# The FFN's residual addition moves from VectorE to a unit-matrix product on TensorE and a ScalarE copy

## The chip, the cores and the metric

The kernel runs on one core of one Trainium2 chip. The metric is the device time of one launch in microseconds (us), taken as the median of several executions. Five engines work side by side, each executing its own instructions in a fixed order and waiting on semaphores for the others: TensorE (PE in the profile), VectorE (DVE), ScalarE (ACT), GpSimd (POOL) and SyncE (SP), which here only issues DMA transfers.

## The reference, cut to what matters

The input x has 8 batches of 512 tokens with 256 channels, all in float32. Four blocks follow one another, each with a residual: a Mamba layer with its feed-forward network (FFN), a gated recurrence over the 8 batches, an attention, and the recurrence again. The change lies in the first block:

```python
h = layernorm(x, ln1_g, ln1_b)
h = h + mamba_mixer(rmsnorm(h, rms_w), ...)
x = x + h
h2 = layernorm(x, ln2_g, ln2_b)
x = x + (jax.nn.relu(h2 @ ffn_w1 + ffn_b1) @ ffn_w2 + ffn_b2)
```

It is the last of these lines: the FFN's second product, 512 tokens by 1024 hidden channels times 1024 by 256, is added to x. The reference's own outer residual adds the input once more, so the kernel's x collects all of it. The recurrence that follows takes the layer norm of this x.

## The kernel before, in words

The work of the first block, together with the first recurrence, fills the first 790 us of the 1630 us and is called the scan stage here. Each batch lies in one SBUF tile `cx.X[b]` of 128 partitions by 4 chunks of 256 channels; a chunk is 128 tokens. The order of nearly everything in the stage is written out by hand: `SLOTS`, `LAST` and `REST` are lists of short names, which `mamba_and_recurrence` walks from left to right, and every engine executes its own share of the resulting stream in that order.

A **period** below is one walk through the 16 slots, numbered by the batch whose scan it contains. In period b the scan of batch b runs (`scan`, `da0`, `da1`, `bx`, `y`, `ld`), and beside it pieces of its neighbours: `i.` and `e.` prepare batches b+1 and b+2, `o.` does the output projection and the FFN of batch b-1, `r.` and `q.` the recurrence of batches b-1 and b-2. Periods 0 to 6 follow `SLOTS`, period 7 follows `LAST`, and `REST` afterwards finishes batch 7 alone, in two halves.

One slot of the scan takes two scans (line 424) and two multiplications (line 428) on VectorE, two exponentials `da` on ScalarE (line 408), and one product `bx` on GpSimd (line 415). The `da` tiles lie in three PSUM banks, so an exponential waits until the scan of three units before has been done.

The FFN of one batch goes like this. `up0` to `up7` are the first product: each is four matmuls of 256 columns (line 517), and `up0_` to `up7_` are its bias and ReLU on ScalarE (line 530, two instructions each). `up0` to `up3` belong to chunks 0 and 1, `up4` to `up7` to chunks 2 and 3. `down0` to `down3` are the second product, one for each chunk of 128 tokens: eight matmuls of 256 columns which add up in one PSUM bank (line 541). `add0` to `add3` add that bank to the chunk of x (line 551), on VectorE. When all four are done, `r.stats` takes the statistics for the recurrence's layer norm (line 70, one instruction for each chunk, then lines 72, 94 and 83), and `r.norm` on ScalarE, `r.turn0`, `r.turn1` and the gates `r.f0` and so on follow. The chunks are worked in the order 1, 0, 3, 2.

Earlier in the same period GpSimd has added the FFN's output bias (`o.bias`, line 479) and the FFN's input (`o.residual`, line 483) to x, so `add` is the last step on x in this block.

The second product, the turns, the gates and the first product share three PSUM banks (tag `mm`); each new product waits until the one that used its bank has been read. In `SLOTS` the pieces around the change stand as follows (slots 8 to 13, shortened):

```python
... i.dt0
da0 o.up3_ i.dt0_ i.soft_exp bx o.down1 da1 o.down0 scan o.add1 ld
ld scan e.outer i.soft_rest da0 o.up4 i.soft_ln o.add0 c.gate0 o.up5 y bx o.up7 o.up4_ da1 o.up6 o.up5_ e.affine o.up6_
i.soft o.up7_ da0 da1 scan bx i.store_dx q.output0 o.down3 o.down2 o.add3 ld
e.square scan da0 o.add2 da1 ld bx y
da0 r.stats q.output0_ q.g1 q.output1 ...
```

Names that come up later: `i.soft_exp` (lines 326 to 328) and `i.soft_ln` (line 337) are ScalarE's part of the next batch's softplus, `i.soft_rest` (lines 332, 333) GpSimd's, and `i.soft` (lines 343, 344) VectorE's; their results are stored and then spread over the partitions by the DMAs `ld`. `e.outer` is four ScalarE instructions (line 106), `e.square` four more (line 205). `c.gate0` is line 453 and 456. `q.output0` and `q.output1` (line 704) exist only in periods 2 and 3. `i.rms` begins with one small VectorE instruction (line 83, tile `ve_a_r`).

Of the kernel before, what the change touches and what calls it, by code (L numbers as in the profile page):

```python
# [87 lines left out]
def layernorm_scales(cx, x, name, scales=((1.0, EPS),)):  # L88

    nc = cx.nc  # L90
    m = x.shape[1]
    mv = token_stats(cx, x, name)
    neg = cx.small.tile([P, TC], F32, tag="neg", name=f"neg_{name}")
    nc.vector.tensor_scalar_mul(neg[:, :m], mv[:, :, 0], -1.0)
    r = inv_sqrt(cx, mv[:, :, 1], scales, name)
    nb = cx.small.tile([P, len(scales), TC], F32, tag=f"nb{len(scales)}", name=f"nb_{name}")
    for i in range(len(scales)):
        nc.gpsimd.tensor_mul(nb[:, i, :m], neg[:, :m], r[:, i, :])
    return [(r[:, i, :], nb[:, i, :m]) for i in range(len(scales))]


def normalize(cx, out, x, scales):

    r, nb = scales
    for c in range(x.shape[1]):
        cx.nc.scalar.activation(
            out[:, c, :], x[:, c, :], AF.Identity, bias=nb[:, c : c + 1], scale=r[:, c : c + 1]
        )


def to_channels(cx, src, k, ps, chunks=range(TC)):

    for i, c in enumerate(chunks):
        cx.nc.tensor.transpose(ps[:, ts(c, P)], src[:, i, ts(k, P)], cx.ident)
    return ps


def part_of(half):

    if half is None:  # L120
        return "", slice(0, L), slice(0, TC)
    tokens, chunks = (slice(half * n // 2, (half + 1) * n // 2) for n in (L, TC))
    return "." + "ab"[half], tokens, chunks
# [322 lines left out]
def mamba_out(cx, a, t, b):  # L446

    nc, v = cx.nc, cx.v
    n = f"o{b}"

    def gate_out(k):

        nc.vector.scalar_tensor_tensor(
            t.y[k], t.xc[:, k, :], v["D"][:, k : k + 1], t.y[k], ALU.mult, ALU.add
        )
        nc.vector.tensor_mul(t.zs[:, k, :], t.zs[:, k, :], t.y[k])

    def proj(i):

        c0 = 2 * i  # L460
        ps = cx.psum.tile([P, 2, E], F32, tag="mm", name=f"ps_op_{n}_{c0}")
        for i in range(2):
            for k in range(KC):
                nc.tensor.matmul(
                    ps[:, i, :],
                    t.zs[:, k, ts(c0 + i, P)],
                    a.out_proj[:, k, :],
                    start=(k == 0),
                    stop=(k == KC - 1),
                )  # L470
        t.proj[c0] = ps

    def add_proj(half):
        for h in range(2) if half is None else [half]:
            u = t.u[:, ts(h, 2), :]
            nc.vector.tensor_add(u, u, t.proj[2 * h])

    def bias():
        nc.gpsimd.tensor_add(t.x, t.x, cx.rows3["ffn_b2"])

    def residual(half):
        cs = part_of(half)[2]
        nc.gpsimd.tensor_add(t.x[:, cs, :], t.x[:, cs, :], t.u[:, cs, :])

    def stats(half):
        t.scales[half] = layernorm_scales(cx, t.u[:, part_of(half)[2], :], n + part_of(half)[0])

    def norm(half):
        if not half:
            t.un = cx.tok.tile([P, TC, E], F32, tag="h", name=f"un_{n}")  # L490
            t.h2 = cx.ch.tile([P, KC, L], F32, tag="T", bufs=3, name=f"h2_{n}")
        cs = part_of(half)[2]
        normalize(cx, t.un[:, cs, :], t.u[:, cs, :], t.scales[half][0])

    def turn(k, half):
        on, _, cs = part_of(half)
        ps = cx.psum.tile([P, L], F32, tag="mm", name=f"ps_h2_{n}_{k}{on}")
        t.ps["h2", k, half] = to_channels(cx, t.un[:, cs, :], k, ps, chunks=range(TC)[cs])

    def turn_(k, half):  # L500
        tk = part_of(half)[1]
        nc.scalar.activation(
            t.h2[:, k, tk],
            t.ps["h2", k, half][:, tk],
            AF.Identity,
            bias=v["b2"][:, k : k + 1],
            scale=v["g2"][:, k : k + 1],
        )

    def up(i):  # L510

        half, m0 = i // 4, i % 4 * 2
        ps = cx.psum.tile([P, 2, L // 2], F32, tag="mm", name=f"ps_f_{n}_{i}")
        t.ps["up", i] = ps
        for m in range(2):
            for k in range(KC):
                nc.tensor.matmul(  # L517
                    ps[:, m, :],
                    a.w1[:, k, ts(m0 + m, P)],
                    t.h2[:, k, ts(half, L // 2)],  # L520
                    start=(k == 0),
                    stop=(k == KC - 1),
                )

    def up_(i):
        half, m0 = i // 4, i % 4 * 2
        if m0 == 0:
            t.f = cx.ch.tile([P, FC, L // 2], F32, tag="f", bufs=1, name=f"f_{n}_{half}")
        for m in range(2):
            nc.scalar.activation(  # L530
                t.f[:, m0 + m, :],
                t.ps["up", i][:, m, :],
                AF.Relu,
                bias=v["ffn_b1"][:, m0 + m : m0 + m + 1],
            )

    def down(c):

        ps = cx.psum.tile([P, E], F32, tag="mm", name=f"ps_f2_{n}_{c}")
        for m in range(FC):  # L540
            nc.tensor.matmul(  # L541
                ps,
                t.f[:, m, ts(c % 2, P)],
                a.w2[:, m, :],
                start=(m == 0),
                stop=(m == FC - 1),
            )
        t.down[c] = ps

    def add(c):  # L550
        nc.vector.tensor_add(t.x[:, c, :], t.x[:, c, :], t.down[c])

    t.proj, t.down, t.scales = {}, {}, {}
    pieces = {"bias": bias}
    for name, f, count in (
        ("gate{}", gate_out, KC), ("proj{}", proj, 2), ("up{}", up, 8), ("up{}_", up_, 8),
        ("down{}", down, TC), ("add{}", add, TC),
    ):
        for i in range(count):
            pieces[name.format(i)] = lambda f=f, i=i: f(i)  # L560
    for half in (None, 0, 1):
        on = part_of(half)[0]
        for f in (add_proj, residual, stats, norm):
            pieces[f.__name__ + on] = lambda f=f, half=half: f(half)
        for name, f in (("turn{}", turn), ("turn{}_", turn_)):
            for i in range(KC):
                pieces[name.format(i) + on] = lambda f=f, i=i, half=half: f(i, half)
    return pieces
# [272 lines left out]
o.bias y o.gate1 o.proj0 o.add_proj.a q.g1 o.stats.a o.residual.a o.norm.a o.proj1 o.turn0.a  # L841
o.turn1.a o.add_proj.b o.turn0_.a o.stats.b o.turn1_.a q.g1_ o.up0 o.norm.b o.up1 q.output1_ o.up2
o.up0_ o.up1_ o.turn1.b o.up3 o.up2_ o.turn1_.b o.up3_ o.turn0.b o.down1 o.down0 o.turn0_.b o.up4
o.residual.b o.up4_ o.up6 q.update1 o.up5 o.up5_ o.up7 o.add1 o.up6_ o.up7_ o.add0 o.down3 o.add3
o.down2 r.stats.a o.add2 r.norm.a r.stats.b
""".strip().split("\n")

# [764 lines left out]
```

## Time and profile before

| what | value |
|---|---|
| median of 3 runs | 1631.15 us (1631.02 to 1632.5) |
| profiled execution | 1632.17 us |
| its span, first to last instruction | 1630.4 us |
| TensorE busy | 1483.8 us (91% of the span) |
| VectorE busy | 1180.8 us (72%) |
| ScalarE busy | 885.2 us (54%) |
| GpSimd busy | 528.7 us (32%) |
| mean granted TensorE clock | 0.95 |

The shares are averages over stages with different limits: from 220 to 580 us both TensorE and VectorE are busy for some 83 to 85 us of every 90, while after 760 us VectorE has little to do. In a timeline each row has the start, the time that the merged instructions took, the engine, the line, the operation, the tiles and the shapes, and in square brackets the idle time before it with what ended it. In a chain each row is one piece of the chain of waits that ended last, with its start and its length. A float32 matmul stands in the records as two instructions.

### The profile page before, as it was taken

Reading aid. Unit: us, or ns where it says so; the run is one execution under the profiler, and the core shown is the slowest. Engines: PE = TensorE matmul, PEld = TensorE weight load, DVE = VectorE, ACT = ScalarE, POOL = GpSimd, SP = SyncE. Lnnn points to the kernel's source line nnn. Section 1 sums busy time; section 2 is a strip of 40 time slices with the busy share of each in tenths; the row PEclk is TensorE's granted clock in tenths of the full one; section 3 lists DMA queues with packets and bytes.
Section 4 is the critical chain, followed back from the end, with each engine's and each line's share of the span. In section 5 each row is a group of like instructions: output and inputs, shape, how many; then the busy total and the mean of one; then the engine's idle time right before and its main releaser. Section 6 shows DMA issues by size and latency. Waiting matters only on the chain.

```text
span 1630.4 us, 19741 instructions
## 1 busy us (share of the span) xinstructions
PE 1483.8 (91%) x6804; PEld 708.6 (43%) x6804; DVE 1180.8 (72%) x1674; ACT 885.2 (54%) x1338; POOL 528.7 (32%) x307
## 2 busy tenths in 40 slices
PE   4347979999999989999989999999999999999998
PEld 1103636455554646456734443333333333333346
DVE  3699998989899898973476867665666657655435
ACT  5775858686767666542235545454444544454422
POOL 2576767767585855541220000000000000000000
PEclk8656989999999999999989999999999999999999
DMA  6979897989989788960211110101010010100123
GB/s 209 254 199 249 205 241 177 281 208 254 245 212 235 206 221 207 227 160 1 107 53 38 43 23 27 27 15 32 13 33 17 26 24 27 27 12 23 29 94 129
DMA packets 111300, 196.04 MB, mean 120 GB/s; under 512 B 16480, under 2 KB 27040, under 8 KB 111200
## 3 DMA queue, kind: packets, MB, share of 16 engines
q1 hardware_dynamic: 108912, 187.79, 44.1%
q10 hardware_dynamic: 1824, 5.15, 0.9%
q0 software_dynamic: 464, 1.84, 0.3%
q8 instruction: 54, 0.88, 0.2%
q14 instruction: 46, 0.38, 0.1%
HBM read 159.06 MB, written 23.07 MB: 112 GB/s over the span
## 4 chain that ended last, share of the span: by engine, by line
PE 64%; DVE 19%; ACT 5%; DMA 5%; issue 4%; POOL 2%; SPq 1%; DVEq 0%; ACTq 0%; POOLq 0%
PE ps_s_c L1111 10%; PE ps_e_c L1111 9%; DVE hc_a L424 8%; PE ps_o_c L1157 8%; DMA dl_rep_a<-dl_dram_a 4%; DVE hc_a L428 3%; PE ps_f_o L517 3%; PE ps_f_o L541 2%; PE ps_v_c L1080 2%; PE ps_w_c L1198 2%; PE ps_f_d L593 2%; PE ps_i_d L593 2%; PE ps_g_d L593 2%; PE ps_f_d L602 2%; PE ps_g_d L602 2%
## 5 line engine op out<-in xcount | busy, mean ns | idle before, releaser
L1122 DVE TENSOR_REDUCE mp<-ps_s_c 128x2 f32<-128x1024 f32 x256 | 301.8, 1220 | 180.1 <-PE ps_s_c L1111 180.1
L1148 ACT ACTIVATE e_c<-ps_e_c 128x1024 f32<-128x1024 f32 x256 | 248.6, 1021 | 166.5 <-PE ps_e_c L1111 166.3
L415 POOL TENSOR_TENSOR bx_a<-dx_rep_a,B_a 128x1024 f32<-128x1024 f32 x128 | 301.6, 2367 | 105.5 <-DVE hc_a L424 68.6
L424 DVE TENSOR_TENSOR_SCAN hc_a<-da_a,bx_a 128x512 f32<-128x512 f32 x256 | 298.2, 1204 | 5.9 <-ACT da_a L408 4.5
L408 ACT ACTIVATE da_a<-dl_rep_a,neg_a 128x512 f32<-128x512 f32 x256 | 173.3, 688 | 147.5 <-DVE hc_a L424 97.0
L1111 PE MATMUL ps_s_c<-keys,q_c 32*128 32x512 f32 x1024 | 176.3, 643 | 2.9 <-ACT q_c L1074 1.2
L1111 PE MATMUL ps_e_c<-q_c,keys 32*128 32x512 f32 x1024 | 164.5, 639 | 2.2 <-DVE mp L1122 2.2
L428 DVE TENSOR_TENSOR hc_a<-hc_a,Cp_a 128x512 f32<-128x512 f32 x256 | 160.7, 667 | 0.0
L1157 PE MATMUL ps_o_c<-e_c,va 128*32 128x512 f32 x1024 | 138.0, 605 | 0.4 <-ACT oT_c L1173 0.3
L84 POOL TENSOR_TENSOR rs_d<-ve_d,neg_half 128x4 f32<-128x4 f32 x8 | 8.1, 1014 | 351.5 <-DVE ve_d L83 351.5
L517 PE MATMUL ps_f_o<-h_o,w 128*128 128x256 f32 x512 | 121.2, 386 | 0.7 <-ACT f_o L530 0.3
L541 PE MATMUL ps_f_o<-w,f_o 128*128 128x256 f32 x512 | 114.2, 381 | 3.8 <-ACT f_o L530 3.8
L437 PE MATMUL y_a<-hc_a,sum 128*32 128x512 f32 x512 | 91.7, 696 | 23.4 <-DVE hc_a L428 15.3
L517 PEld LDWEIGHTS ps_f_o<-h_o,w 128*128 128x128 f32 x512 | 96.6, 192 | 35.0 <-issue 10.3
L541 PEld LDWEIGHTS ps_f_o<-w,f_o 128*128 128x128 f32 x512 | 96.3, 190 | 22.9 <-ACT f_o L530 5.4
L1111 PEld LDWEIGHTS ps_s_c<-keys,q_c 32*128 32x128 f32 x1024 | 57.3, 183 | 94.3 <-issue 39.4
L84 POOL TENSOR_TENSOR rs_c<-ve_c,neg_half 128x4 f32<-128x4 f32 x7 | 7.1, 1009 | 264.9 <-DVE ve_c L83 264.9
L1111 PEld LDWEIGHTS ps_e_c<-q_c,keys 32*128 32x128 f32 x1024 | 50.9, 183 | 93.7 <-issue 59.8
L240 PE MATMUL ps_in_a<-hT_a,w_in 128*128 128x512 f32 x128 | 69.6, 683 | 1.1 <-ACT hT_a L235 1.1
L530 ACT ACTIVATE f_o<-ps_f_o,vecs 128x256 f32<-128x256 f32 x128 | 52.1, 468 | 23.0 <-PE ps_f_o L517 20.2
L1157 PEld LDWEIGHTS ps_o_c<-e_c,va 128*32 128x32 f32 x1024 | 20.4, 108 | 90.0 <-issue 78.5
L1190 DVE RECIPROCAL sum_c<-sum_c 128x256 f32<-128x256 f32 x32 | 55.7, 1742 | 1.2 <-DMA sum_c<-oT_c 1.2
(327 smaller groups left out, 2146.8 us busy)
## 6 DMA issues: line engine op xcount, KB each, us to landing
dl_rep_a<-dl_dram_a SPq DMA_DIRECT2D x256, 256.0 KB, 6.4
dx_rep_a<-dx_dram_a SPq DMA_DIRECT2D x256, 256.0 KB, 6.4
x<-in_x_dram SPq DMA_DIRECT2D x8, 512.0 KB, 9.6
keys<-xT_c SPq DMA_DIRECT2D x128, 32.0 KB, 1.9
o_c<-oT_c SPq DMA_DIRECT2D x128, 32.0 KB, 1.9
sum_c<-oT_c SPq DMA_DIRECT2D x128, 32.0 KB, 2.0
xT_dram_d<-xT_d SPq DMA_DIRECT2D x8, 512.0 KB, 2.8
xT_back<-xT_dram_d SPq DMA_DIRECT2D x8, 512.0 KB, 5.5
```

Source lines behind the costliest of these rows:

```text
L408: cx.nc.scalar.activation(t.da[u], t.dl_rep[u // 2][:, u % 2, :], AF.Exp, scale=a.A[:, u : u + 1])
L415: cx.nc.gpsimd.tensor_mul(t.bx[pair], t.dx_rep[pair], t.B.unsqueeze(1).to_broadcast([P, 2, L]))
L424: cx.nc.vector.tensor_tensor_scan(t.hc[u], t.da[u], t.bx[pair][:, u % 2, :], 0.0, ALU.mult, ALU.add)
L428: cx.nc.vector.tensor_mul(t.hc[u], t.hc[u], t.Cp)
L437: cx.nc.tensor.matmul(t.y[k][head(j), :], a.sum[:, r, :], t.hc[4 * quad + j], start=(r == 0), stop=(r == QR - 1),)
L517: nc.tensor.matmul(ps[:, m, :], a.w1[:, k, ts(m0 + m, P)], t.h2[:, k, ts(half, L // 2)], start=(k == 0), stop=(k == KC - 1),)
L541: nc.tensor.matmul(ps, t.f[:, m, ts(c % 2, P)], a.w2[:, m, :], start=(m == 0), stop=(m == FC - 1),)
L593: cx.nc.tensor.matmul(ps[:, tk], cx.gw[:, g, k, ts(m, P)], xT[:, k, tk], start=(k == 0), stop=False)
L1111: cx.nc.tensor.matmul(ps[:, i, :], lhs[rows, :], rhs[rows, :], start=True, stop=True)
L1122: cx.nc.vector.tensor_reduce(c.mp[:, t, h : h + 2, DH], ps, AX.X, ALU.max, negate=True)
L1148: cx.nc.scalar.activation(e, ps, AF.Exp)
L1157: cx.nc.tensor.matmul(po[head(j), :], c.va[b % 2][:, t, g * HG + j, :], es[j // 2][:, j % 2, :], start=(t == 0), stop=(t == TC - 1),)
```

## The change

The second product gains one matmul ahead of its eight: the 128 by 128 unit matrix, which the kernel keeps for its transposes, times the chunk of x. It starts the sum in the bank, so the bank ends as x plus the product. The piece `add` becomes a copy of that bank to x on ScalarE. In `REST` the pieces `add1` and `add0` stand further to the left; `SLOTS` and `LAST` are as before, so there each copy takes the addition's place in the list, but in ScalarE's order instead of VectorE's.

```diff
     def down(c):
         ps = cx.psum.tile([P, E], F32, tag="mm", name=f"ps_f2_{n}_{c}")
+        nc.tensor.matmul(ps, cx.ident, t.x[:, c, :], start=True, stop=False)
         for m in range(FC):
             nc.tensor.matmul(
                 ps,
                 t.f[:, m, ts(c % 2, P)],
                 a.w2[:, m, :],
-                start=(m == 0),
+                start=False,
                 stop=(m == FC - 1),
             )
         t.down[c] = ps

     def add(c):
-        nc.vector.tensor_add(t.x[:, c, :], t.x[:, c, :], t.down[c])
+        nc.scalar.copy(t.x[:, c, :], t.down[c])
...
 REST:
-o.residual.b o.up4_ o.up6 q.update1 o.up5 o.up5_ o.up7 o.add1 o.up6_ o.up7_ o.add0 o.down3 o.add3
+o.residual.b o.up4_ o.add1 o.add0 o.up6 q.update1 o.up5 o.up5_ o.up7 o.up6_ o.up7_ o.down3 o.add3
```

## The prediction, made before the changed kernel ran

> **What bounds the kernel now.** I read first the table of busy time by stretches, then the chain of waits, then each engine's timeline around the second product. Its row for 310 to 400 us, whose columns are busy time and instruction counts of TensorE, its weight loads, VectorE, ScalarE and GpSimd, then TensorE's clock, the DMA share and GB/s:
>
> ```profile
> 310.00:400.00 90.00, 85.24 (x335) 49.13 (x333) 84.55 (x126) 66.48 (x116) 63.07 (x32) 0.98 0.89 239
> ```
>
> TensorE and VectorE are both busy for some 85 of 90 us, so neither has room to spare and the chain must say which one counts where. In period 2 it runs, from the second `dt` product on, over TensorE alone:
>
> ```profile
> 265.99 1.05 PE ps_dt_a L298 x2
> 267.04 7.10 PE ps_f_o L541 x32
> 274.15 3.45 PE ps_f_o L517 x16
> 277.60 1.00 PE y_a L437 x8
> 278.60 3.65 PE ps_f_o L517 x16
> 282.25 1.73 PE ps_o_b L704 x8
> 283.97 3.47 PE ps_f_o L541 x16
> 287.46 0.04 DVE x L551
> ```
>
> Before these rows (from 243 us) it is also TensorE, back to the turn of the normalized FFN input; after them it is VectorE, from the additions over the statistics to that turn in the next period. So a period in the middle is a ring: VectorE from the statistics to the convolution, then TensorE from the turn through `down2`. Period 3 has the same pattern; the two engines' timelines there:
>
> ```profile
> 352.96 7.17 PE L541 MATMUL ps_f_o<-w,f_o 128*128 128x256 f32 x32
> 369.80 7.07 PE L541 MATMUL ps_f_o<-w,f_o 128*128 128x256 f32 x32
> ...
> 356.72 0.42 DVE L551 TENSOR_TENSOR x<-x,ps_f_o 128x256 f32<-128x256 f32 x1 [3.15 <-PE ps_f_o L541]
> 364.12 2.58 DVE L343 TENSOR_TENSOR dl_a<-dl_a,w_a 128x1024 f32<-128x1024 f32 x1 [1.84 <-ACT w_a L337]
> 377.21 0.41 DVE L551 TENSOR_TENSOR x<-x,ps_f_o 128x256 f32<-128x256 f32 x1
> 377.55 1.40 DVE L70 BATCH_NORM_STATS2 st_b<-x 128x6 f32<-128x256 f32 x4
> ```
>
> Here `down1` and `down0` are the 32 records at 352.96, `down3` and `down2` those at 369.80. VectorE waits 3.15 us for `down1`, then for softplus; the last addition starts at 377.21 without a wait, only 0.34 us after TensorE's end at 376.87. That 0.34 us is all the slack of TensorE in periods 2 and 3. From period 4 on `q.output0` (1.73 us) is gone, and TensorE ends 2.0 us ahead of the last addition (455.45 + 7.07 = 462.5, against 464.47). In period 1 it is 2.3 us (201.8 against 204.15). In `REST`, from 754 us to `down2`'s end at 782.07, the chain is TensorE almost without a break.
>
> **What the Trainium skill says.** "TensorE: Matmul & The Clock Gate", Part 1, has TensorE's clock halved after a mostly idle window of some 3.4 us, the windows running freely, and restored after a busy one. The trace agrees: in period 4 TensorE idles 2.6 us before the turn of the recurrence's input, and the clock then is 0.5 for two such stretches:
>
> ```profile
> 469.75 2.80 PE L114 MATMUL ps_xT_b<-ident,xn_b 128*128 128x128 f32 x8 [2.60 <-ACT xn_b L106]
> 469.80:473.20 3.40, 3.32 (x9) 1.89 (x10) 3.37 (x5) 2.83 (x6) 3.40 (x3) 0.50 0.90 233
> 473.20:476.60 3.40, 3.40 (x5) 1.28 (x4) 3.40 (x5) 0.92 (x2) 3.40 (x2) 0.50 1.02 242
> ```
>
> The same page, "Architectural detail", calls ScalarE and VectorE strictly first in, first out: a copy that waits holds what is behind it. The rows of the trace stand in program order and agree. "SBUF — State Buffer", section on its two sides, says that VectorE and GpSimd lock each other out of a shared port for a whole instruction. The tiny `ve_a_r` of `i.rms` shows it:
>
> ```profile
> 480.11 1.92 DVE L83 TENSOR_SCALAR ve_a_r<-ms_a 128x4 f32<-128x4 f32 x1
> ```
>
> In period 3 it takes 0.30 us; here it ends with a `bx` of GpSimd that runs from 479.64 to 482.01. `dl_a` and `dx_a` (2.58 and 3.28 us), too, end on GpSimd's boundaries.
>
> **The change part by part.**
>
> *Unit products.* The trace before has none of the kind, but its shape is that of the eight beside it. The four runs at 352.96 and 359.97 give 7.01 us for 16 matmuls, 0.44 us each; four in a batch are 1.75 us, 32 in all 14 us. They cost nothing where TensorE idles anyway, and 0.44 us each where it doesn't; a bound above would be 0.5 us. The copy of x is read once GpSimd's `o.residual` is done, which ends at 337.4 in period 3, 15 us ahead of `down1`; in `REST` at 751.4 and 756.6, against 761 and 775. No wait comes from there.
>
> *Additions removed.* 32 rows of 0.41 us, 0.33 us from start to start: 10.6 us of VectorE. `add1` and `add0` lie in front of the wait for softplus (364.12), so what they free, and the 3.15 us wait, only lengthens that wait. `add3` and `add2` lie between `dx_a` and the statistics and are worth 0.66 us where VectorE is the bound. Besides, the statistics of chunks 0 and 1 no longer stand behind `add2`: 0.66 us of them can run while VectorE waits for it.
>
> *Copies added.* The nearest row is ScalarE's copy of the same shape out of PSUM,
>
> ```profile
> 787.52 0.37 ACT L651 COPY xT_b7.a<-ps_xT_b7.b 128x256 f32<-128x256 f32 x1 [1.50 <-PE ps_xT_b7.b L114]
> ```
>
> 0.37 us; the ReLU rows of 0.47 us bound it above. `add1` stands after `da` (358.98), when `down1` is done, and pushes `e.outer` and `soft_ln` by 0.3 us. `dl_a` starts later but gains nothing by starting earlier: it ends behind GpSimd's `bx` of 363.25 to 365.62, which waits for neither. So 0. `add0` stands after `soft_ln` (364.4) and frees the bank for `up7`, which TensorE reaches at 365.4: 0. `add3` waits about 1 us for `down3`; behind it stand `e.square` and `da`, needed by a scan 5 us later: 0. SP's and GpSimd's queues lose and gain no instruction.
>
> *Period 1*: VectorE is the bound before and after: -0.66.
>
> *Periods 2 and 3*: `down2` ends at 376.87 + 1.75 = 378.62, its copy at 379.03. The third statistics instruction waits for it; before it started at 377.55 + 0.66 = 378.21. So +0.82 each, +1.64.
>
> *Periods 4 and 5*: `down2` ends at 464.25, the copy at 464.65; VectorE needs it at 464.80, its time less 0.66 and plus the two early statistics. It fits with 0.15 us: -0.66 each, -1.32.
>
> *Period 6*: also -0.66 up to the statistics. But the tanh of gate g, which stands before `r.norm` on ScalarE, now waits for TensorE's 1.75 us, and behind the turn VectorE waits 3.43 us for TensorE (658.89). Taken as 0, bounds -1.0 and +0.3.
>
> *Period 7*: TensorE idles 2.03 us before 712.63, waiting for a ReLU that DMA holds up; three unit products vanish in it. The fourth moves the end from 717.23 to 717.67, both copies to 718.4, the last two statistics to about 718.75. Before they ended at 719.24: -0.5.
>
> *REST*: four unit products, +1.75. `up6` now takes the bank of `up4`, not of `down1`, and starts only when both ReLU instructions have read it (0.84 us and a signal): +0.95. `add2` stands before `r.norm.a` on ScalarE, so that norm, which ran beside `down2` at 781.44, now follows it: from `down2`'s end to the first transpose a copy and a first norm chunk (0.37 + 0.59, so 1.0 us) in place of 0.6 us, and the second transpose of the pair waits for its own chunk: +0.4 to +0.9, taken as 0.55. Sum +3.25, with nothing behind it that waits.
>
> Sum: -0.66 + 1.64 - 1.32 + 0 - 0.5 + 3.25 = **+2.4 us**. The profiled execution took 1632.17 us (span 1630.4 and 1.8 around it), so 1634.6; the median of the runs lies 1.0 lower, so 1633.5.
>
> **The rivals.**
>
> *The clock stays up in periods 4 and 5 (faster).* The idle time before the turn shrinks from 2.6 us to some 1.2 us. If no window is then idle enough, the gate product ends 2 us earlier, VectorE doesn't wait 0.58 us for it, and `ve_a_r` meets the `bx` before, as in period 3: from statistics to next scan 14.86 us there (377.55 to 392.41), 17.14 here (464.80 to 481.94). That is -2.3 us in each, -1.0 in period 6: 2.4 - 4.6 - 1.0 = -3.2, 1627.9 us. Against it: in the 3.4 us from the idle's start the turns still wait for norm chunks, and are half idle.
>
> *TensorE becomes the bound in periods 4 to 6 too (slower).* The slack of 0.15 us is the point that decides. The place is the TensorE chain from the turn to `down2`, whose clock is halved after the turn for one or two windows (329.9 to 333.3 in one period, 415.2 to 422.0 in the next); a window more costs 1.7 us. Every shift moves the windows. Three periods at +0.8 in place of -0.66 or 0, with one window more, give 2.4 + 1.5 + 1.5 + 0.8 + 1.7 = +7.9, so 1639.
>
> *The freed VectorE shows (faster).* 10.6 us off an engine that is 94% busy would be 1620.6; the wait for softplus and the ring speak against it. It stays a small part of the faster side.
>
> **How the numbers follow.** 0.2% of 1631 is 3.3 us, about what a measurement of this kernel can tell from no change. The forecast, +2.4 or the same with part of the clock's gain, stays within it: 0.42. TensorE as the bound in more periods: slower, 0.36. The clock's whole gain, or more of VectorE's: faster, 0.22. Time 1633.5; the range from 1626.5 to 1639 takes in the clock's gain with some of VectorE's, and the slower rival.
>
> **What would show it.** Right: VectorE's wait at the additions gone, that before `dl_a` near 6 us; in periods 2 and 3 two statistics, a gap of about 1.2 us, two more; `down2` some 1.75 us later relative to `down1`; 0.9 us idle on TensorE before `up6` in `REST`, and the chain there 3.2 us longer. Wrong: gaps before the statistics in periods 4 to 6 as well, a clock of 1.0 through the gates there, or a shorter stretch from statistics to statistics in periods 2 and 3.

## The result, and the profile after

The changed kernel takes 1637.16 us (median; 1632.13 to 1641.92) against 1630.46 us for the kernel before in the same comparison: ratio 1.0041, 95% interval 1.0029 to 1.0054. It is slower by 6.7 us. The forecast was 1633.5, 2.4 us more than before. The measured time lies inside its range (1626.5 to 1639), but beyond the 0.2% within which the likeliest case would have kept it.

The busy times by stretch again, with the columns as in the prediction:

```profile
310.00:400.00 90.00, 84.17 (x332) 49.23 (x331) 81.88 (x120) 64.89 (x115) 61.42 (x32) 0.98 0.85 226
```

Both engines are busy for less of the 90 us than before (84.2 and 81.9 against 85.2 and 84.6), though TensorE has more to do: the periods that lie there, 2 and 3, became longer (from turn to turn 90.0 and 89.1 us, against 87.1 and 86.0). In period 2 the chain of waits is the same one, with the unit products (line 540) in it:

```profile
265.47 0.63 PE ps_f_o L540 x2
266.10 3.45 PE ps_f_o L542 x16
269.55 0.43 PE ps_f_o L540 x2
...
287.58 3.45 PE ps_f_o L542 x16
291.03 1.00 PE y_a L437 x8
292.03 1.91 PE ps_g_b L594 x4
293.94 1.73 PE ps_g_b L603 x4
295.68 0.02 issue
295.70 0.67 ACT ps_g_b L609
296.37 0.02 issue
296.39 0.71 DVE ps_g_b L693
```

New is where it leaves TensorE. Before, that was at an addition; now it is further on, over the tanh of gate g on ScalarE to VectorE's first use of that gate (line 693). The timelines of VectorE and TensorE in period 3 answer those of the prediction:

```profile
365.97 2.29 DVE L343 TENSOR_TENSOR dl_a<-dl_a,w_a 128x1024 f32<-128x1024 f32 x1 [5.97 <-ACT w_a L337]
378.33 0.74 DVE L70 BATCH_NORM_STATS2 st_b<-x 128x6 f32<-128x256 f32 x2
380.61 0.75 DVE L70 BATCH_NORM_STATS2 st_b<-x 128x6 f32<-128x256 f32 x2 [1.54 <-ACT x L552]
376.12 0.59 PE L540 MATMUL ps_f_o<-x,ident 128*128 128x256 f32 x2
376.55 3.62 PE L542 MATMUL ps_f_o<-w,f_o 128*128 128x256 f32 x16
```

These are signs that the prediction named: 5.97 us of waiting ahead of `dl_a`, two statistics, a gap (1.54 us, where it said about 1.2), two more. So the change did what it says. To see where the rest of the time went, every period is cut at three marks which both kernels have: the turn `ps_h_o`, the start of `down1` (with its unit product), and the end of the fourth `st_b`. Each number is the distance of two rows in the trace of one profiled execution (1632.17 us before, 1639.69 after), in us:

| stretch | before | after | difference | forecast |
|---|---|---|---|---|
| down1 to the statistics' end, period 1 | 27.89 | 27.15 | -0.74 | -0.66 |
| the same, periods 2 and 3, each | 25.98 | 26.83 | +0.85 | +0.82 |
| the same, periods 4, 5, 6 | 25.85, 25.86, 25.86 | 25.19, 25.22, 25.18 | -0.66, -0.64, -0.68 | -0.66 each |
| statistics' end to the next turn, periods 1 to 2 | 35.34 | 35.36 | +0.02 | 0 |
| the same, 2 to 3 and 3 to 4 | 35.37, 35.39 | 37.69, 37.70 | +2.32, +2.31 | 0 |
| the same, 4 to 5 and 5 to 6 | 37.66, 37.67 | 37.69, 37.68 | +0.04 together | 0 |
| the same, 6 to 7 | 33.04 | 34.58 | +1.54 | +0.66 |
| turn to down1, periods 1 to 6, sum | 150.4 | 150.2 | -0.2 | 0 |
| period 7, turn to the statistics' end | 44.17 | 44.75 | +0.6 | -0.5 |
| REST, from there to the first turn of batch 7 | 63.34 | 66.67 | +3.33 | +3.25 |
| before period 1's turn, and after the stage | | | -1.4 | 0 |

The rows add up to the 7.5 us by which the two profiled spans differ; the medians differ by 6.7 (the table's +0.66 for 6 to 7 is the forecast's 0 for the period, less its -0.66 for the statistics). The largest item, 4.6 us, is one that the forecast has at zero. It is a tiny instruction, `ve_a_r`. VectorE, with `ve_b` as the mark to count from, and then GpSimd around the end of period 2, before:

```profile
293.35 0.16 DVE L83 TENSOR_SCALAR ve_b<-mv_b 128x4 f32<-128x4 f32 x1
...
306.21 0.28 DVE L83 TENSOR_SCALAR ve_a_r<-ms_a 128x4 f32<-128x4 f32 x1
...
304.10 2.36 POOL L415 TENSOR_TENSOR bx_a<-dx_rep_a,B_a 128x1024 f32<-128x1024 f32 x1
```

and after, with the wait for gate g nine microseconds earlier:

```profile
292.62 0.16 DVE L83 TENSOR_SCALAR ve_b<-mv_b 128x4 f32<-128x4 f32 x1
...
296.39 0.70 DVE L693 SCALAR_TENSOR_TENSOR ps_g_b<-act_i_b,ps_g_b 128x512 f32<-128x512 f32 x1 [0.20 <-ACT ps_g_b L609]
305.77 2.31 DVE L83 TENSOR_SCALAR ve_a_r<-ms_a 128x4 f32<-128x4 f32 x1
...
303.37 2.39 POOL L415 TENSOR_TENSOR bx_a<-dx_rep_a,B_a 128x1024 f32<-128x1024 f32 x1
305.69 2.37 POOL L415 TENSOR_TENSOR bx_a<-dx_rep_a,B_a 128x1024 f32<-128x1024 f32 x1
```

Count from `ve_b`, the last instruction of the statistics' arithmetic, for which GpSimd waits: the `bx` that starts at 304.10 before and at 303.37 after ends 13.1 us after it in both kernels. VectorE reaches `ve_a_r` 12.86 us after it before and 13.15 us after it now. It is some 0.02 us late for the end of that `bx`, and comes out at the end of the next one, at 15.46: 0.28 us became 2.31. "SBUF — State Buffer", in the section on its two sides, has GpSimd and some of VectorE's instructions locking each other out for a whole instruction; a 4-column instruction that takes 2.31 us, and ends each time with a `bx`, agrees with it. What made it late is visible too: 0.20 us of waiting for gate g (0.29 us with the overlap of neighbouring instructions that the wait breaks), which TensorE computes after `down2` and one `y`. The statistics now end 1.19 us after `down2` instead of 2.07 (the copy and two early statistics), so VectorE gets to the gate sooner after `down2` than before, and the gate isn't there.

From period 6 to 7 no lock is involved. ScalarE, then VectorE:

```profile
648.42 0.66 ACT L609 ACTIVATE ps_g_b<-ps_g_b,gate_b 128x512 f32<-128x512 f32 x1 [1.05 <-PE ps_g_b L603]
...
663.29 0.76 DVE L453 SCALAR_TENSOR_TENSOR y_a<-xc_a,vecs,y_a 128x512 f32<-128x512 f32 x1 [3.74 <-PE y_a L437]
```

The tanh of gate g waits for TensorE and holds the norm behind it, so the recurrence's turn starts 4.68 us after the statistics instead of 3.55, and VectorE then waits for a `y` that TensorE computes behind that turn and two gates. Here TensorE bounds the period from `down1` to the next turn: 58.90 us before, 59.76 after. TensorE's clock moves this stretch as much as the change does. Two rows of busy time behind that turn, of the changed kernel and of e8 (an experiment below, whose code is the same up to there), with the clock as the third number from the end:

```profile
652.30:655.70 3.40, 3.40 (x5) 1.29 (x6) 3.40 (x5) 1.57 (x3) 3.40 (x2) 0.50 0.93 266
646.40:649.80 3.40, 3.16 (x8) 1.29 (x8) 3.40 (x5) 2.09 (x4) 3.40 (x2) 1.00 0.91 242
```

In e8 the clock stays up, and the stretch from 6 to 7 is 33.15 us. Of the profiles with 3.4 us at half clock in it, those with the old code there have 33.04 to 33.24 us and those with the change 34.05 to 34.60; with 6.8 us at half clock the old code has 33.98 (e7 and e9).

In period 7, TensorE and then ScalarE:

```profile
708.70 3.50 PE L517 MATMUL ps_f_o<-h_o,w 128*128 128x256 f32 x15 [2.48 <-ACT x L552]
...
707.65 0.69 ACT L408 ACTIVATE da_a<-dl_rep_a,neg_a 128x512 f32<-128x512 f32 x1 [3.11 <-DVE hc_a L424]
708.28 0.63 ACT L552 COPY x<-ps_f_o 128x256 f32<-128x256 f32 x2
```

`up4` and `up6` need the banks of `down0` and `down1`. The two copies that free them stand behind an exponential `da`, which waits 3.11 us for a scan, and TensorE idles 2.48 us for them.

In `REST` the forecast's items are all there, TensorE first:

```profile
776.79 5.45 PE L517 MATMUL ps_f_o<-h_o,w 128*128 128x256 f32 x24 [0.99 <-ACT f_o L530]
790.97 0.33 PE L114 MATMUL ps_xT_b7.a<-ident,xn_b7.a 128*128 128x128 f32 x1 [0.96 <-ACT xn_b7.a L106]
...
790.05 0.37 ACT L552 COPY x<-ps_f_o 128x256 f32<-128x256 f32 x1 [3.46 <-PE ps_f_o L542]
790.32 1.09 ACT L106 ACTIVATE xn_b7.a<-x,nb_b7.a,rs_b7.a 128x256 f32<-128x256 f32 x2
```

0.99 us of idle time for `up4_`, and 0.96 us from `down2` to the turn, where it was 0.61, so +0.35. The end of `down2` itself comes 2.98 us later; with the four unit products at 1.72 us the wait for `up4_` is worth 1.26: its idle time and, what no run shows apart, probably the ends of the matmuls around it.

### The profile page after: what moved, and what is told of

It is laid out like the page before. It is cut to its first block, busy times and chain, and to the rows that moved or that the text cites. A ratio compares the mean times of both kernels' runs of the same rounds, so it can differ in the third digit from the quotient of the medians.

```text
span 1637.9 us, 19886 instructions
## 1 busy us (share of the span) xinstructions
PE 1486.4 (91%) x6868; PEld 717.4 (44%) x6868; DVE 1171.2 (72%) x1642; ACT 894.9 (55%) x1370; POOL 529.3 (32%) x307
## 4 chain that ended last, share of the span: by engine, by line
PE 72%; DVE 16%; ACT 4%; DMA 3%; issue 2%; POOL 1%; SPq 1%; DVEq 0%; ACTq 0%; POOLq 0%
PE ps_s_c L1112 10%; PE ps_e_c L1112 9%; PE ps_o_c L1158 8%; DVE hc_a L424 7%; PE ps_f_o L517 6%; PE ps_f_o L542 5%; DVE hc_a L428 3%; PE y_a L437 2%; PE ps_v_c L1081 2%; PE ps_w_c L1199 2%; PE ps_f_d L594 2%; PE ps_i_d L594 2%; PE ps_g_d L594 2%; PE ps_f_d L603 2%; PE ps_g_d L603 2%
```

## The experiments

All ratios are to the kernel before, with 95% intervals; 0.001 is 1.6 us. Single stretches come from one profile each. Most of those of periods 2 to 5 and of `REST` repeat to 0.03 us from kernel to kernel. Those from the turn to `down1`, from period 6 to 7 and in period 7 don't: TensorE's half-clock stretches fall differently there each time. That is why a stretch settles more here than a total.

### Taking the lock away: e1 and e2

In both, the small instruction of `i.rms` is executed by GpSimd itself, in e1 in the changed kernel, in e2 in the kernel before:

```diff
 def inv_sqrt(cx, v, scales, name):
+    side = nc.gpsimd if name.startswith("a") and name.endswith("_r") else nc.vector
     for i, (scale, eps) in enumerate(scales):
-        nc.vector.tensor_scalar(ve[:, ts(i, m)], v, scale, eps, ALU.mult, ALU.add)
+        side.tensor_scalar(ve[:, ts(i, m)], v, scale, eps, ALU.mult, ALU.add)
```

> The changed kernel, with the one small VectorE instruction of i.rms (tile ve_a_r) moved to GpSimd, so that it cannot wait for the end of a GpSimd product. Theory A (the loss is largely that this instruction now misses the end of one bx and waits for the next, 2.31 us in periods 2 and 3 in place of 0.28 and 0.30): its times over 0.2 us, 1.2 + 2.1 + 2.1 + 1.7 + 1.2 = 8.3 us in the changed kernel, go, so about 1629 us against 1637.2, and the stretch from the end of the statistics to the next turn ps_h_o is the same 35.4 us in periods 2 to 5. Theory B (TensorE's added 14 us is the loss, VectorE's wait lies beside it): within 1 us of 1637.2. Theory C (TensorE's half-clock stretches decide): the stretch from the turn to down1 moves by 1 to 3 us in single periods, with no fixed sign.

> The kernel before with the same move of ve_a_r to GpSimd. Theory A: 1.0 + 0.1 + 0.1 + 1.7 + 2.0 = 4.9 us of waiting go, so about 1625.6 us against 1630.5, and the distance between this kernel and the changed one with the same move is 3 to 3.5 us in place of 6.7. Theory B: within 1 us of 1630.5, and the distance stays near 6.7 us. Theory C: either sign, by up to 3 us.

Measured: e1 0.9988 (0.9979 to 0.9998), against 1.0041 for the changed kernel, so about 8.6 us less, where 8.3 was expected. e2 0.9978 (0.9969 to 0.9986), 3.6 us less, where 4.9 was expected. The distance between the two falls from 6.7 to about 1.6 us, give or take 2, so it may be nothing or the 3 to 3.5 us expected. The four stretches from the statistics' end to the next turn, periods 2 to 6, add up to 150.8 us in the changed kernel and 142.9 in e1, and to 146.1 before and 142.6 in e2: the sums account for both times. GpSimd in e2, period 4:

```profile
475.22 6.97 POOL L416 TENSOR_TENSOR bx_a<-dx_rep_a,B_a 128x1024 f32<-128x1024 f32 x3
482.27 0.19 POOL L84 TENSOR_SCALAR ve_a_r<-ms_a 128x4 f32<-128x4 f32 x1
```

On GpSimd it takes 0.19 us, behind the last product. It ends 15.7 us after `ve_b` there, later than in the changed kernel (15.46), and the stretch is 2.2 us shorter all the same: what cost time was VectorE held at its place, not a late result. Theory A holds, though the stretches in e1 are not all equal (35.46, 35.46, 35.86 and 36.13 us). For B (TensorE's 14 us) and C (the clock) there remains what is left between e1 and e2.

### The same lock by one place in the order: e10

```diff
 SLOTS:
-da0 y a.take_c bx i.rms i.scale scan q.g0 ...
+da0 y bx i.rms a.take_c i.scale scan q.g0 ...
```

> The changed kernel with i.rms one VectorE instruction earlier, ahead of the copy of C (line 316); bx keeps its place in front of it on GpSimd. Nothing is added or removed. If ve_a_r only waits for the end of the bx that it falls into, starting 0.6 us earlier lets it catch the end that it misses by under 0.1 us: 0.6 us at most in place of 2.31 in periods 2 and 3, the copy of C right behind it at its 0.68 us, and the stretch from the statistics' end to the next turn falls from 37.7 to 35.4 us in periods 2 and 3. Sum -4 to -5 us, ratio 1.001. If the wait has another reason (a semaphore, a dependency on GpSimd's queue), it takes as long as before, plus 0.6: ratio 1.004.

```profile
306.26 0.60 DVE L83 TENSOR_SCALAR ve_a_r<-ms_a 128x4 f32<-128x4 f32 x1
306.77 0.68 DVE L316 COPY Cp_a<-C_a 128x512 f32<-128x512 f32 x1
...
302.13 7.01 POOL L415 TENSOR_TENSOR bx_a<-dx_rep_a,B_a 128x1024 f32<-128x1024 f32 x3
```

The instruction, 0.6 us earlier, catches the `bx` end that it missed: 0.60 and 0.58 us in periods 2 and 3. That part of the expectation is met, and the wait is shown to depend on the moment, not on a semaphore or on GpSimd's queue, both of which the edit leaves as they were. The stretch falls to 35.99 and 35.96 us, not to 35.4: the copy of C, which stood ahead of the lock, now comes behind it. In periods 4 and 5, where even the earlier start is too late, the same copy makes it 38.27 us. My sum of 4 to 5 us had left that out; by the stretches 1.7 + 1.7 - 0.6 - 0.6 - 0.6 = 1.6 us remain, and 1.0028 (1.0016 to 1.0041), 2.1 us less than the changed kernel, fits that, though the two intervals overlap and the time alone wouldn't show it.

### Which half of the change brings the lock: e5 and e6

```diff
 e5, no unit product:
-        nc.tensor.matmul(ps, cx.ident, t.x[:, c, :], start=True, stop=False)
...
-                start=False,
+                start=(m == 0),
 e6, unit product, VectorE copies, REST in its old order:
-        nc.scalar.copy(t.x[:, c, :], t.down[c])
+        nc.vector.tensor_copy(t.x[:, c, :], t.down[c])
```

> The changed kernel without the unit products: ScalarE copies the bank to x, so x is left out of the sum (the copy and all orders stay). It shows what the move from VectorE to ScalarE does alone. Theory A (ve_a_r misses its bx in periods 2 and 3 because the gate g, on TensorE after down2 and its y, now lags the statistics, which the copy and the two early statistics have brought closer to down2's end; VectorE waits 0.2 us for that gate): the statistics come 0.66 us earlier in periods 1 to 6 and down2 ends 1.75 us earlier than in the changed kernel, so the gate is in time again, ve_a_r takes 0.3 us in periods 2 and 3, and the sum is 6 x -0.66, about -1 in period 7 and 3.34 - 1.75 = +1.6 in REST: 3 us below the kernel before, ratio 0.998. Rival (the missing additions alone shift VectorE against GpSimd): ve_a_r still takes 2.3 us in periods 2 and 3, ratio 1.001.

> The unit products stay, but VectorE copies the bank to x in the place of its addition, and REST has its old order. It shows what TensorE's 14 us do alone. Theory A: the statistics again stand behind the copy of down2, so from down2's end to the statistics' end it is 2.07 us in periods 2 and 3 and the gate g doesn't lag them; ve_a_r 0.3 us there. TensorE's slack of 0.34 us in periods 2 and 3 goes: +1.4 each; in periods 1, 4 and 5 it has 2 us: 0; period 6 up to the next turn +0.9; period 7's wait for a ReLU hides it: 0; REST +1.75. Sum +5.5 us, ratio 1.0034, and REST from the statistics of period 7 to the first turn 63.34 + 1.75 = 65.1 us. Rival (the later down2 by itself makes ve_a_r miss): ve_a_r 2.3 us in periods 2 and 3 as in the changed kernel, +10 us, ratio 1.006.

e6: 1.0036 (1.0022 to 1.0050), and `REST` 65.06 us; both as expected. `down1` to the statistics' end is 27.41 us in periods 2 and 3, +1.43. VectorE doesn't wait for gate g, and `ve_a_r` is in time (in period 5 too, 0.28 us, which was not expected and shortens the stretch there by 2.3 us in this profile):

```profile
298.27 0.69 DVE L693 SCALAR_TENSOR_TENSOR ps_g_b<-act_i_b,ps_g_b 128x512 f32<-128x512 f32 x1
...
307.64 0.29 DVE L83 TENSOR_SCALAR ve_a_r<-ms_a 128x4 f32<-128x4 f32 x1
```

e5, whose sum leaves x out: 0.9985 (0.9972 to 0.9998), the expected time, but not by the expected way:

```profile
291.87 0.70 DVE L692 SCALAR_TENSOR_TENSOR ps_g_b<-act_i_b,ps_g_b 128x512 f32<-128x512 f32 x1 [0.20 <-ACT ps_g_b L608]
...
301.25 2.31 DVE L83 TENSOR_SCALAR ve_a_r<-ms_a 128x4 f32<-128x4 f32 x1
```

Without a unit product `ve_a_r` still takes 2.31 us in period 2 (and 1.75 in period 3, where that stretch is 37.70 us again), with the same 0.20 us for gate g. My theory had the later `down2` as half of the reason; that half is wrong, and on this wait the rival was right. The lag behind gate g follows from how soon after `down2` the statistics end: 1.19 us in e5 as in the changed kernel, 1.77 in e6, 2.07 before. What e5 gained instead was in periods 4 and 5, where `ve_a_r` caught its `bx` (0.27 and 0.31 us), which was not expected: 35.37 and 35.39 us from the statistics to the turn, against 37.66 and 37.67 before. There TensorE's clock stayed up behind the turn, where it was 0.50 before,

```profile
470.40:473.80 3.40, 3.40 (x8) 1.06 (x6) 3.40 (x5) 1.43 (x3) 3.40 (x3) 1.00 1.03 259
```

and VectorE's wait for gate f ahead of `ve_a_r` (0.58 and 0.28 us before) is gone. That is the mechanism of the prediction's faster rival. So in periods 2 and 3 the move of the operation from VectorE to ScalarE, and not the product on TensorE, brings the lock.

### Where the loss lies: e3, e4, e8 and e11

e3 and e4 apply the change to some batches only:

```diff
+        unit = b < B - 1        # e3; in e4: b >= B - 2
+        if unit:
             nc.tensor.matmul(ps, cx.ident, t.x[:, c, :], start=True, stop=False)
...
-        nc.scalar.copy(t.x[:, c, :], t.down[c])
+        if unit:
+            nc.scalar.copy(t.x[:, c, :], t.down[c])
+        else:
+            nc.vector.tensor_add(t.x[:, c, :], t.x[:, c, :], t.down[c])
```

> The change for batches 0 to 6 alone; batch 7 (REST) adds on VectorE, without unit products, in the old order. If REST costs what was forecast (3.25 us) and has nothing to hide it: 1633.9 to 1634.2 us against 1637.2. If the loss of REST is mostly a shift of what comes later and is given back in the attention: within 1 us of 1637.2.

> The kernel before with the change for batches 6 and 7 alone (period 7 and REST). If the middle periods 1 to 6 carry about half of the loss (their direct gain of 4 us against 4.6 us of waiting of ve_a_r and 2.3 us of half clock): 1630.5 + 0.7 + 3.0 = about 1634.2 us. If the middle periods are a gain or nothing, and period 7's copies behind the waiting exponentials are the loss: 1636 to 1638 us. If period 7 gains 0.5 us as forecast: 1633.2.

e3: 1.0033 (1.0023 to 1.0043), only 1.3 us under the changed kernel, with an interval of some 2.5 us either way; the time doesn't decide it. Its trace does: `REST` is back at 63.34 us, and the other stretches show the lock unchanged (37.70 and 37.69 us). e4: 1.0023 (1.0014 to 1.0033), so 3.7 us, as the first theory has it, with `REST` at 66.68 us; the interval takes in the third case (1633.2 us) too. In its profile period 7 gains 1.1 us (43.04 against 44.17), which is the sign that the prediction gave: TensorE doesn't idle for the copies there. In e1, e3 and e8 it does, 1.33, 3.08 and 2.75 us: whether the exponential ahead of the copies is late probably depends on how the scans stand to TensorE by then, which no run isolates. One profile says little about period 7 as a whole: with the old code in it, it took 43.66 us in e7 and 46.16 in e9.

e8 and e11 move pieces of the changed kernel:

```diff
 e8, REST:
-o.residual.b o.up4_ o.add1 o.add0 o.up6 ... o.down2 r.stats.a o.add2 r.norm.a r.stats.b
+o.residual.b o.add1 o.add0 o.up4_ o.up6 ... o.down2 r.stats.a r.norm.a o.add2 r.stats.b
 e11, LAST:
-o.down0 da0 bx scan o.down1 ld o.up4 da1 c.gate0 o.add0
-o.add1 da0 scan ...
+o.down0 da0 bx scan o.down1 ld o.up4 o.add0 o.add1 da1 c.gate0
+da0 scan ...
```

> The changed kernel with two moves in REST: the copies of down1 and down0 ahead of up4's ReLU, and the first norm ahead of the copy of down2. If up6's wait for up4's ReLU is worth 0.95 us and the norm behind the copy 0.55 us, as forecast, the stretch from the statistics of period 7 to the first turn of batch 7 falls from 66.68 to 65.2 us, and what is left over 63.34 is the four unit products, 1.75 us. If the copies only move the wait to up4's ReLU: no less than 66.2 us.

> The changed kernel with one move in LAST: the copies of down0 and down1 ahead of the exponential da1 of slot 9. If TensorE's idle time of 1.3 to 3.1 us ahead of up4 and up6 of period 7 is the copy that stands behind an exponential which waits for a scan, it goes, and from the turn of period 7 to the statistics' end it is 43.0 us, as in the kernel with the change for the last two batches alone (43.04), in place of 44.75. Ratio 1.002 to 1.003. If the copies only trade places with the exponentials and the scans come later for it: 44.5 us or more, ratio 1.004.

e8: 1.0030 (1.0014 to 1.0045). `REST` takes 64.91 us: TensorE goes through all of `up6`, `up5`, `up7` and what follows without a break, and the turn comes 0.46 us after `down2`.

```profile
769.02 7.07 PE L517 MATMUL ps_f_o<-h_o,w 128*128 128x256 f32 x32
...
784.33 0.66 PE L114 MATMUL ps_xT_b7.a<-ident,xn_b7.a 128*128 128x128 f32 x4 [0.46 <-ACT x L552]
```

Of the 3.33 us, 1.76 were the order of the pieces (1.26 at `up6`, 0.50 at the turn) and 1.57 remain: the four unit products, less 0.15 us at the turn. e11: 1.0035 (1.0023 to 1.0047). The idle time ahead of the `up` products is gone, but TensorE then waits 1.30 us for a ReLU in `down3`, and period 7 takes 44.15 us, between the 43.0 and the 44.5 expected, so neither case is confirmed:

```profile
705.24 3.62 PE L517 MATMUL ps_f_o<-h_o,w 128*128 128x256 f32 x16
...
716.10 1.13 PE L542 MATMUL ps_f_o<-w,f_o 128*128 128x256 f32 x4 [1.30 <-ACT f_o L530]
```

### What can be had: e7, e9 and e12

All three have `ve_a_r` on GpSimd. e7 and e9 make the change in batches 0 to 4 and in batches 0, 3 and 4 (by `unit = b <= 4` and `unit = b in (0, 3, 4)` in the edit of e3); e12 makes it everywhere, with the moves of e8 and e11.

> The kernel before with ve_a_r on GpSimd, and the change for batches 0 to 4 alone (periods 1 to 5). Theory A: it leaves out what loses for sure (period 6's wait for y, +0.9; the copies behind waiting exponentials in period 7, 0 to +1.2; REST, +3.3), and gains 0.7 in periods 1, 4 and 5 against 0.85 in 2 and 3: 1 us or so below the kernel before with ve_a_r on GpSimd, up to 5 us below if TensorE's clock stays up in periods 4 and 5 as in the changed kernel with ve_a_r on GpSimd (from the turn to down1 23.2 us there, 24.6 and 26.0 here). Ratio 0.995 to 0.997. Rival (the clock takes back what the ring gains): 0.998 or above.

> The kernel before with ve_a_r on GpSimd and the change for batches 0, 3 and 4 alone (periods 1, 4 and 5), where TensorE has 2 us of slack. By the measured stretches from down1 to the statistics' end, -0.7 us in each of the three, and 0.85 us less in each of periods 2 and 3 than with the change there: 1.7 us below the kernel with the change in batches 0 to 4, ratio 0.995 against its 0.9962. Rival (a difference of 1.7 us is lost in the half-clock stretches that each execution has elsewhere): 0.996 to 0.998.

> The change in all batches with what was found about it mended: ve_a_r on GpSimd, the copies ahead of the exponential in LAST, the copies ahead of up4's ReLU and the first norm ahead of the last copy in REST. Against the changed kernel with ve_a_r on GpSimd (0.9988): 2.1 us less in REST (its turn ends at 65.57 us after period 7's statistics in place of 67.70) and about 1.3 us less in period 7: ratio 0.9967, which would be below the kernel before with ve_a_r on GpSimd (0.9978). If the orders only shift waits: 0.9985 or more.

e7: 0.9962 (0.9950 to 0.9974), 6.2 us under the kernel before and the lowest ratio of this study. It beats the kernels before and after the change; its interval overlaps those of e2, e9 and e12. e9: 0.9978 (0.9967 to 0.9989). Its stretches are as expected (27.12 us in period 1, 25.99 and 25.98 in 2 and 3, 25.21 and 25.20 in 4 and 5), but the expected gain over e7 isn't in the time; the two intervals overlap, so the rival, that a difference of 1.7 us is lost in the clock, is not contradicted. e12: 0.9978 (0.9968 to 0.9989). `REST` (the turn ends 65.58 us after the statistics) and period 7 (42.00 us) are as expected or better, and yet it isn't shown faster than e2. With these waits mended, the change in every batch gains nothing that these runs can show over moving one 4-column instruction.

## Why the prediction was right, and where it wasn't

**The time.** The direction is right. That the time lies inside the range is in part luck: the likeliest time was 3.7 us too low, and the range reached up to 1639 for a rival that did not occur.

**The ring and the direct cost.** Right, to 0.1 us in each row: VectorE the bound from `down1` to the statistics in periods 1 and 4 to 6, TensorE in 2 and 3 (-0.74, +0.85, -0.64 to -0.68). The slack of 0.15 us in periods 4 to 6 was enough; the statistics there have no gap.

**The softplus wait, unit products and copies.** Right: `down1` to `down2`'s end grew by 1.72 us in periods 2 to 6 (1.75 forecast), a copy takes 0.37 us, and the wait ahead of `dl_a` is 5.97 us ("near 6"). One reading was wrong without harm: `dl_a` and `dx_a` do not end on GpSimd's boundaries but 1.1 us after them (366.70 and 370.02, behind ends at 365.62 and 368.92). `dl_a` still ends behind that `bx` after the change, so the term of 0 stands.

**REST.** Right: +3.33 for +3.25, as 1.72 + 1.26 + 0.35 (1.75, 0.95 and 0.55 in the forecast). The transposes end another 0.40 us later relative to it, so the norm behind the copy costs 0.75 us in all, where 0.55 was taken.

**Statistics to the next turn, periods 2 and 3.** The step that failed. The prediction took VectorE's path from the statistics to the turn as unchanged, though it had quoted the two states of `ve_a_r` itself. It used them only for a gain in its faster rival, and didn't ask how close the state without a wait was to the other: 0.25 us (12.86 against 13.1), with a shift of 0.29 us coming. That is +4.6 us in the profile. e1 and e2 show it, e10 shows that the moment decides, e5 and e6 that the move to ScalarE shifts it.

**Period 6.** Probably mis-sized: taken as 0 with bounds of -1.0 and +0.3, it is +0.86 from `down1` to the next turn in the profile. The wait of gate g's tanh and VectorE's wait for `y` had both been named; that makes TensorE the bound there, and TensorE has 1.75 us more to do. But the clock moves this stretch by as much: it is 58.32 us in e8, with the same code and the clock up, and 59.84 in e7 with the old code. Among profiles with 3.4 us at half clock the change costs 0.1 to 0.9 us.

**Period 7.** The gain of 0.5 us isn't in the changed kernel's profile (+0.6). Three unit products vanish in idle time only when the copies come in time, as in e4 (-1.1); in the changed kernel TensorE idles 2.48 us for the copies. For this period the prediction didn't ask what stands ahead of the copies on ScalarE.

**The rivals.** The slower one gives nearly the measured time (1639) by the wrong mechanism: in periods 4 to 6 TensorE didn't become the bound ahead of the statistics, only behind them in period 6. The mechanism of the faster one exists, as e5 shows in periods 4 and 5, but in the changed kernel VectorE still waits 0.44 and 0.80 us for gate f there. The clock ahead of `down1` doesn't explain the result: the stretches from turn to `down1` sum to 125.0, 127.0, 121.2 and 122.3 us over periods 2 to 6 in the profiles of the changed kernel, e3, e8 and e11, whose code is the same up to there, and to 125.3 in the kernel before. How much of the total's 6.7 us is owed to periods 6 and 7, which vary likewise, stays open.

## What to carry to other kernels

Moving an operation to another engine moves the moments of everything behind it: where an instruction shares a port with another engine's long ones, look how far from the boundary it stands, since 0.02 us too late cost 2.3 us here in each of two periods. For a moved operation, read what stands ahead of it in its new queue, too: a copy that frees a bank is as late as the wait in front of it. Small instructions whose duration varies in the profile are worth moving off the path first; here that one edit gained 3.6 us, half as much as the whole change cost.

## What the hardware showed beyond that

`ve_a_r` works on 4 columns. On VectorE it took 0.17 us with no `bx` under way. With one under way it took 0.16 to 2.33 us in the nine runs that leave it there, and in each of these 54 cases it ended 0.02 to 0.05 us after a `bx` did. On GpSimd it took 0.19 us. Its like, `ve_b`, took 0.16 us while GpSimd waited for it.

A half-clock stretch doesn't need TensorE to be idle all the time before it. The prediction quotes "TensorE: Matmul & The Clock Gate", Part 1, with a "mostly idle" window; the page says an idle window. In the 3.4 us ahead of the half-clock stretch of period 4 that the prediction shows, TensorE was busy for 0.81 us:

```profile
466.39:469.80 3.41, 0.81 (x3) 0.06 (x1) 3.38 (x8) 1.90 (x4) 2.89 (x3) 1.00 1.06 293
```

So a window idle only in part was enough; how idle it must be, these runs don't tell. Nor are the half-clock stretches fixed by the code. After one and the same program up to period 6, the first 6.8 us from its turn ran at half clock in the changed kernel's profile and at full clock in e8's:

```profile
594.10:600.90 6.80, 5.93 (x19) 2.42 (x19) 6.73 (x9) 4.80 (x7) 2.61 (x3) 0.51 0.96 225
```

```profile
591.40:598.20 6.80, 5.93 (x26) 2.75 (x27) 6.73 (x9) 5.19 (x7) 2.61 (x3) 1.00 1.02 255
```

From the turn to `down1` it was 25.82 us in the one and 23.06 in the other. The same page and part has the windows that decide this run freely, not reset when a kernel starts, which agrees. It also means that one profile can't judge a change of 2 us here unless it is read by stretches.
